# Closing groups of rows inside a symmetric attention layer instead of after it

## The chip, the cores and the metric

The kernel runs on one core of one Trainium2 chip. The metric is the device time of one execution in microseconds (us), taken as the median of several runs. TensorE is called PE, VectorE DVE, ScalarE ACT, GpSimd POOL and SyncE SP, as the profile does. Matmuls are in fp32, and each shows as two records (two passes); a transpose through PE is one pass.

## The reference

Four images of 64 x 64 pixels and 64 channels go through four layers:

```python
x = _L0_conv_ref(x, ...)   # attention over 4096 pixels, q = xWq, k = xWk, v = xWv
x = _L1_conv_ref(x, ...)   # norm, pointwise, depthwise 3x3, gates, residuals
x = _L2_conv_ref(x)        # attention without weights, see below
x = _L3_conv_ref(x, ...)   # non-local block: theta, phi, g of 32 channels, batch norm, residual
```

Layer 2 reads its input as `B, C, H, W = x.shape`, so what it takes for channels is the image's first spatial axis and its tokens are the 64 x 64 pairs of the last two axes:

```python
xf = x.reshape(B, C, N)
scores = jnp.einsum('bci,bcj->bij', xf, xf)
attn = jax.nn.softmax(scores, axis=-1)
out = jnp.einsum('bcj,bij->bci', xf, attn).reshape(B, C, H, W)
return out + x
```

Its score matrix is symmetric: query and key are the same vectors. Layer 3 is

```python
f = jax.nn.softmax(jnp.einsum('bnd,bmd->bnm', theta_x, phi_x), axis=-1)
y = jnp.einsum('bnm,bmd->bnd', f, g_x).reshape(B, H, W, INNER)
w_y = jnp.einsum('bhwd,dc->bhwc', y, w_W) + w_b
return x + w_y_normalised_over_batch_and_pixels
```

so the normalisation needs all four images, and the finish comes after the last of them.

## The kernel before

One list of items is built for the whole program, and a driver emits item after item. Each item writes its instructions into the engines' queues, so the order in the list is the order on every engine; engines wait for each other by semaphores. Beside the items there are three ways to insert work: `at(i, fn)` emits a function after item i; generators under `conv` and `misc` emit one step whenever the items' declared times (`conv.tick`, `misc.tick`) have added up to what the step asks by its `yield`; and `small` emits a function within an item of layer 3.

The order of the stages is: layer 0 of four images, with layer 1 spread between; layer 2 of image 0 in its full form; then in turn the symmetric layer 2 of an image (72 items) and layer 3 of the image before it (64 items); last, layer 3 of images 2 and 3 back to back, and the finish. All intermediate results stay on the chip.

**Symmetric layer 2** (`layer2s`). The 4096 tokens form eight groups of 512. A block is the scores of one group against another. Since the matrix is symmetric, a block between two different groups is computed once and used twice. `SIDES` says which group h does the blocks with which other groups, two at a time (a pair, four items). An item is one 128 x 1024 half of such a block: `score` (PE, L1432, into a two-bank slot of PSUM), the exponentials with row sums (ACT, L1437), and for a block off the diagonal a 32 x 32 block transpose (DVE, `turned`, L1449) and column sums (POOL, L1460). `products` (PE, L1484) come two items later; after a pair, `turned_products` (PE, 128 records, L1500) use the transposed half with weights loaded by 16 SP DMAs per group (`weights`, L1415), and DVE adds the result into the accumulator `A` (`add_to`, L1474). Scores rotate over three slots of two banks each; two more banks hold the products. `spread_sums` (DVE, L1468, L1469) turns POOL's column sums.

When all 72 items are done, an image is closed: `close2s` sums the row sums and column sums of all groups (four matmuls L1550, DVE L1552 to L1556), transposes `A` through PE (four times eight transposes, L1561) and adds the scaled result to `X` on DVE (L1562, L1568). Its five steps are inserted at items 8, 12, 22, 32 and 42 of the next image's symmetric layer; for image 3, as a generator in layer 3 of image 2. Image 0 is closed by `close2`, from item 2 of image 1's symmetric layer on, DVE only (L1372 to L1379).

**Layer 3.** `open3` makes theta (L1588), phi (L1599) and g (L1607), each into a slot of two banks, and `keys3` spreads phi by 16 SP DMAs (L1622). An item of `layer3` is 16 score records (L1643) into four banks of seven that rotate, exponentials on ACT (L1654), and products two items later (L1700) into the eighth bank. Denominators are summed on DVE (L1691) or, for eight items in each half of 32, by POOL's accumulating DMAs (L1671, L1673). After each half come `totals` (L1712, L1736) and a reciprocal (L1728 to L1730), and then `close` with the projection (L1750), ACT (L1763) and statistics (L1765). `features2` (L1300, L1303) transposes the next image's `X` for its layer 2, in two parts of eight transposes, each in two banks.

Of the kernel before, what the change touches and what calls it, by code (L numbers as in the profile page):

```python
# [691 lines left out]
def fast_path(ctx: ExitStack, tc: tile.TileContext, a: dict, out: bass.AP, bad):  # L692
# [42 lines left out]

    def take_slots(*slots):
        turn_of["slots"], turn_of["ps"], turn_of["banks"] = list(slots), 0, 0
# [144 lines left out]
    sel4 = const.tile([128, 32], F32, name="sel4")  # L882
    pwb = const.tile([128, 2, 2], F32, name="pwb")
# [22 lines left out]
    def setup():  # L906
# [33 lines left out]
        for i in range(4):  # L940
# [5 lines left out]
            yield 4.0  # L946
        nc.vector.tensor_add(sel4, ident[:, 0:32], ident[:, 32:64])
# [345 lines left out]
    def features2(b):  # L1293
# [3 lines left out]
        for g in range(2):  # L1297
            ps = new_ps()
            for i in range(8):
                nc.tensor.transpose(ps[:, bass.ts(i, 128)], x[:, bass.ts(8 * g + i, 128)], ident)  # L1300
            for e, copy in enumerate((nc.vector.tensor_copy, nc.scalar.copy)):
                own, other = slice(64 * e, 64 * e + 64), slice(64 - 64 * e, 128 - 64 * e)
                copy(kv[own, bass.ts(g, 8), e, :], ps[own, :].rearrange("p (a n) -> p a n", n=128))  # L1303
                nc.sync.dma_start(out=kv[other, bass.ts(g, 8), e, :], in_=kv[own, bass.ts(g, 8), e, :])
            yield 7.0

    def layer2(b):
# [7 lines left out]
        def scores(n):  # L1315
# [3 lines left out]
            for jb in range(4 * (n % 8), 4 * (n % 8) + 4):  # L1319
# [13 lines left out]
                conv.tick(2.3)  # L1333
# [51 lines left out]
    SIDES = [[(7, (h + 1) % 7), ((h + 2) % 7, (h + 3) % 7)] for h in range(7)] + [[]]  # L1385

    def layer2s(b, when_free):
# [7 lines left out]
        for h in (7, 0, 1, 2, 3, 4, 5, 6):  # L1395
# [3 lines left out]
                for pi, pair in enumerate(SIDES[h]) for gi, g in enumerate(sorted(pair)) for u in range(2)  # L1399
            ]  # L1400
            steps += other + own if h == 6 else own + other
        st = {"e": {}, "T": {}, "esum": {}}

        def slot(g, t):
            k = used[g, t] = used.get((g, t), -1) + 1
            c = 16 * g + 4 * t if g < 7 else 112 + 8 * t
            return m.zs[:, c + k : c + k + 1]
# [34 lines left out]
        def turned(n):  # L1442
# [3 lines left out]
            if ti == 0 and pi not in st["T"]:  # L1446
                st["T"][pi] = new_big("turned")
            T = st["T"][pi].rearrange("p (e s j) -> p s e j", e=16, s=8)
# [4 lines left out]
        def column_sums(n):  # L1453
# [7 lines left out]
            if (pi, ti) == (1, 3):  # L1461
# [30 lines left out]
        def turned_products(h, pi):  # L1492
            T, slots = st["T"][pi], [new_ps(), new_ps()]
# [11 lines left out]
            for i in range(2):  # L1505
                for gi, g in enumerate(sorted(SIDES[h][pi])):
# [11 lines left out]
        def item(n):  # L1518
            h = steps[n][0]
            if n >= 4 and steps[n - 4][0] == h and (n == 4 or steps[n - 5][0] != h):  # L1520
                weights(h)
# [11 lines left out]
            if n - 2 in last_of:  # L1533
                turned_products(*last_of[n - 2])
                if last_of[n - 2] == (6, 0):
                    when_free()
            if n - 5 in last_of and last_of[n - 5][1] == 1:
                spread_sums(last_of[n - 5][0])

# [5 lines left out]
    def close2s(b):  # L1545
# [509 lines left out]
```

## Time and profile before

| | us |
|---|---|
| median of 3 runs (2470.71 to 2475.36) | 2475.31 |
| the profiled execution | 2475.64 |
| its span | 2473.9 |
| PE busy in the span | 2431.5 (98%) |
| ACT busy | 1642.7 (66%) |
| DVE busy | 1428.7 (58%) |
| POOL busy | 506.8 (20%) |

Stages, in us from the span's start: layers 0 and 1 to about 1016; layer 2 of image 0 to 1271; symmetric layer 2 of image 1 from 1274 to 1474, layer 3 of image 0 to 1611, symmetric layer 2 of image 2 to 1808, layer 3 of image 1 to 1946, symmetric layer 2 of image 3 to 2143, layer 3 of image 2 to 2300, layer 3 of image 3 to about 2443, and the finish.

How to read it: shares are of the whole span, and a stage can have another bound than the sum. "Idle before" names what ended an engine's idleness. A group's mean is of one instruction; matmuls run beside each other on parts of the array, so the distance from one start to the next is a better price than the length. The granted clock is the TensorE clock that the throttle let through, 1.00 being full speed; over the whole span it was 0.996.

### The profile page before, as it was taken

The page shows a single profiled execution, that of the slowest core. Times are in us where ns is not written, and L with a number is a line of the kernel's source. Part 1 is how long each engine was busy: PE and PEld are TensorE (multiplying, and loading weights), DVE is VectorE, ACT ScalarE, POOL GpSimd, SP SyncE. Part 2 cuts the span into 40 slices and gives each one's busy share as a digit, 9 for nine tenths or more (in the row PEclk, how much of TensorE's full clock was granted, in tenths as well). Part 3 has the DMA queues.
Part 4 walks back from the last instruction along what each step waited for, and adds up shares of the span by engine and source line. Part 5 has one row for each costly group of instructions (what it writes and reads, how often), then busy time and mean ns, then how long its engine had stood idle before and what let it go on. Part 6 is the DMA issues. An engine that isn't in the chain of part 4 may idle for free.

```text
span 2473.9 us, 62215 instructions
## 1 busy us (share of the span) xinstructions
PE 2431.5 (98%) x27037; PEld 925.5 (37%) x27037; DVE 1428.7 (58%) x1701; ACT 1642.7 (66%) x2979; POOL 506.8 (20%) x345
## 2 busy tenths in 40 slices
PE   9999999999999999999989999999999999999998
PEld 3343453336433643344324442134431244421123
DVE  2010277228822782267335558877668876687886
ACT  4666766667666766666645459954479744569996
POOL 2000000000000000000007661256631366512110
PEclk9999999999999999999999999999999999999999
DMA  3000000010000000000000027610075400376554
GB/s 79 1 18 1 18 1 18 18 19 1 18 18 18 1 18 18 18 2 18 18 18 19 19 48 151 138 27 21 18 148 116 81 21 22 73 139 127 118 118 119
DMA packets 59151, 115.33 MB, mean 47 GB/s; under 512 B 11149, under 2 KB 30326, under 8 KB 58870
## 3 DMA queue, kind: packets, MB, share of 16 engines
q0 software_dynamic: 19136, 67.68, 13.7%
q1 hardware_dynamic: 38981, 41.75, 7.5%
q8 instruction: 214, 3.51, 0.6%
q10 hardware_dynamic: 752, 1.85, 0.2%
q14 instruction: 68, 0.55, 0.1%
HBM read 4.80 MB, written 4.19 MB: 4 GB/s over the span
## 4 chain that ended last, share of the span: by engine, by line
PE 88%; DVE 5%; ACT 4%; DMA 1%; issue 1%; SPq 0%; POOL 0%; DVEq 0%; ACTq 0%; POOLq 0%
PE PS L1116 18%; PE PS L1090 17%; PE PS L1643 8%; PE PS L1700 8%; PE PS L1432 7%; PE PS L1484 7%; PE PS L1500 6%; PE PS L1323 4%; PE PS L1343 4%; PE PS L1200 2%; DVE tg L1691 2%; ACT e L1654 2%; DMA xn<-e 1%; ACT e L1095 1%; PE PS L1165 1%
## 5 line engine op out<-in xcount | busy, mean ns | idle before, releaser
L1095 ACT ACTIVATE e<-PS 128x1024 f32<-128x1024 f32 x512 | 523.7, 1023 | 331.3 <-PE PS L1090 299.2
L1116 PE MATMUL PS<-e,vq 64*64 64x512 f32 x4096 | 573.8, 591 | 0.0
L1090 PE MATMUL PS<-X,q 64*64 64x512 f32 x4096 | 571.6, 591 | 1.8 <-DVE X L974 1.7
L1654 ACT ACTIVATE e<-PS 128x512 f32<-128x512 f32 (+2 forms) x593 | 500.4, 915 | 66.9 <-PE PS L1643 42.8
L1437 ACT ACTIVATE e<-PS 128x512 f32<-128x512 f32 x432 | 253.5, 594 | 289.6 <-PE PS L1432 270.9
L1691 DVE TENSOR_TENSOR tg<-tg,e 128x2048 f32<-128x2048 f32 x174 | 398.6, 2291 | 49.4 <-ACT e L1654 37.0
L1233 DVE SCALAR_TENSOR_TENSOR y<-pad,vec,y 128x1024 f32<-128x1024 f32 x240 | 308.1, 1284 | 7.5
L1460 POOL TENSOR_TENSOR esum<-esum,e 128x1024 f32<-128x1024 f32 x126 | 298.9, 2372 | 58.6 <-ACT e L1437 51.5
L1643 PE MATMUL PS<-tg,ph 32*64 32x512 f32 x4096 | 300.3, 615 | 6.5 <-DVE A L1474 3.3
L1090 PEld LDWEIGHTS PS<-X,q 64*64 64x64 f32 x4096 | 184.4, 133 | 257.3 <-issue 178.8
L1116 PEld LDWEIGHTS PS<-e,vq 64*64 64x64 f32 x4096 | 184.6, 133 | 251.3 <-issue 152.9
L1700 PE MATMUL PS<-e,tg 128*32 128x512 f32 x2048 | 273.5, 606 | 0.0
L1449 DVE STREAM_TRANSPOSE turned<-e 128x1024 f32<-128x1024 f32 x168 | 206.7, 1239 | 79.8 <-ACT e L1437 79.7
L1484 PE MATMUL PS<-e,X 64*64 64x512 f32 x1728 | 232.7, 594 | 6.2 <-DVE A L1474 6.1
L1432 PE MATMUL PS<-ko 64*64 64x512 f32 x1728 | 235.4, 598 | 0.0
L1528 POOL MEMSET A<- 128x4096 f32 x3 | 11.2, 3736 | 1012.5 <-PE PS L1116 1012.5
L1103 DVE TENSOR_REDUCE sums<-zs 128x1 f32<-128x4 f32 x128 | 19.6, 153 | 301.3 <-ACT e L1095 300.9
L1331 ACT ACTIVATE e<-PS 128x1024 f32<-128x1024 f32 x128 | 129.6, 1023 | 83.7 <-PE PS L1323 80.4
L1500 PE MATMUL PS<-turned,xn 32*64 32x256 f32 x5376 | 157.2, 377 | 2.5 <-DVE sums L1554 1.6
L1673 POOL DMA_DIRECT2D xn<-e x112 | 97.6, 906 | 294.4 <-ACT e L1654 201.1
L1474 DVE TENSOR_TENSOR A<-PS,A 128x256 f32<-128x256 f32 (+1 forms) x216 | 92.5, 477 | 105.2 <-PE PS L1500 80.7
L1643 PEld LDWEIGHTS PS<-tg,ph 32*64 32x64 f32 x4096 | 65.4, 130 | 227.7 <-ACT e L1654 175.8
(224 smaller groups left out, 1927.4 us busy)
## 6 DMA issues: line engine op xcount, KB each, us to landing
xn<-e POOLq DMA_DIRECT2D x128, 512.0 KB, 5.3
xn<-X SPq DMA_DIRECT2D x336, 32.0 KB
xn<-t SPq DMA_DIRECT2D x64, 128.0 KB
ph<-tg SPq DMA_DIRECT2D x64, 128.0 KB
ko<-ko SPq DMA_DIRECT2D x16, 256.0 KB
xr<-in_x_dram SPq DMA_DIRECT2D x13, 256.0 KB
q<-q SPq DMA_DIRECT2D x12, 256.0 KB
out_dram<-o SPq DMA_DIRECT2D x7, 256.0 KB
```

What stands on the lines that cost most here:

```text
L1090: mm(ps[64 * c : 64 * c + 64, bass.ts(r, 512)], m.q[rows_, 128 * t + 64 * c : 128 * t + 64 * c + 64], x[rows_, bass.ts(g, 512)], start=Tru ...
L1095: act(es[g // 2][:, bass.ts(g % 2, 1024)], ps, AF.Exp, bias=SHIFT0, accum_out=zs[:, g : g + 1],)
L1116: ins = mm(PS[64 * s : 64 * s + 64, 2048 + 512 * j : 2560 + 512 * j], vq[rows_, :], es[j // 2][rows_, k : k + 512], start=t == 0 and i < 2 ...
L1233: stt(y1, win, wt, y1, ALU.mult, ALU.add)
L1432: mm(ps[64 * c : 64 * c + 64, bass.ts(r, 512)], m.ko[rows_, k : k + 64], m.ko[rows_, bass.ts(h, 512)], start=True, stop=True,)
L1460: nc.gpsimd.tensor_add(esum, st["e"][n - 1] if (pi, ti) == (0, 1) else esum, st["e"][n])
L1484: mm(st["acc"][r][64 * c : 64 * c + 64, :], xw[rows_, jb, :], st["e"][n][rows_, bass.ts(c, 512)], start=n == mine[0], stop=n == mine[-1],)
L1500: mm(slots[q // 2][64 * c : 64 * c + 64, o : o + 256], st["xr"][rows_, w : w + 64], T[rows_, bass.ts(e, 256)], start=e < 2, stop=e >= 14,)
L1643: mm(PS[64 * c : 64 * c + 64, bass.ts(banks[k], 512)], m.ph[32 * k : 32 * k + 32, 128 * mc + 64 * c : 128 * mc + 64 * c + 64], m.th[32 * k ...
L1654: act(e[:, 512 * lo : 512 * k], PS[:, 512 * banks[lo] : 512 * banks[lo] + 512 * (k - lo)], AF.Exp,)
L1691: nc.vector.tensor_add(esum, esum, e)
L1700: mm(st["y"][32 * k : 32 * k + 32, :], m.gx[:, i % 32, :], es[i][:, bass.ts(k, 512)], start=mc == 0, stop=i % 32 == 31,)
```

## The change

**Pairs.** `SIDES` is another table: groups 0 to 3 each do blocks with groups 4 to 7 and so finish earlier; there are still 28 blocks off the diagonal in 14 pairs. `COUNT` and `FIRST` lay out the row sums by group.

**Closing by groups.** `close2s` is replaced by `close_group(b, g)`, eight calls per image. Its first step sums the group's row sums on DVE and, for seven of the eight groups, column sums by four small matmuls into columns 256 to 260 of one PSUM piece, which DVE adds. Then four matmuls of `A` with `fold2` go into columns 0 to 256 of the same piece: `fold2` is two stacked 64 x 64 identities, so that a transpose and the sum of the two halves are one matmul. DVE scales and adds into `X`, four times 64 columns. Groups 1, 0, 2, 3 and 5 are closed within the image's own symmetric layer (items 38, 50, 53, 61 and 71), groups 4, 6 and 7 at items 6, 9 and 12 of the next image's, or, for image 3, in layer 3 of image 2.

**Insertions in one bank.** `piece()` gives one bank in layer 3 (and half a slot elsewhere). `open3`, `close`, `features2` and `totals` take pieces: theta in two, phi in two, g in two, close in two halves, features in four. In layer 3 they are emitted right after an item's exponentials, cut 1024 + 1024 there, not 512 + 1536 (`between3`, `cut`).

**Smaller moves.** `weights` is issued in the item before a group begins; `close2(0)` moves from item 2 to items 16, 17, 30 and 31 of image 1's symmetric layer; `conv.tick` in layer 2 is 2.5 instead of 2.3.

The core of the diff:

```diff
...
+    def piece():
+        if turn_of["banks"]:
+            return PS[:, bass.ts(new_bank(), 512)]
+        return new_ps()[:, 0:512]
+
     def take_slots(*slots):
...
     sel4 = const.tile([128, 32], F32, name="sel4")
+    fold2 = const.tile([128, 64], F32, name="fold2")
     pwb = const.tile([128, 2, 2], F32, name="pwb")
...
             yield 4.0
+        nc.vector.tensor_add(fold2, ident[:, 0:64], ident[:, 64:128])
         nc.vector.tensor_add(sel4, ident[:, 0:32], ident[:, 32:64])
...
         kv = ko[:, 0:N].rearrange("p (a e n) -> p a e n", e=2, n=128)
-        for g in range(2):
-            ps = new_ps()
-            for i in range(8):
-                nc.tensor.transpose(ps[:, bass.ts(i, 128)], x[:, bass.ts(8 * g + i, 128)], ident)
+        for g in range(4):
+            ps = piece()
+            for i in range(4):
+                nc.tensor.transpose(ps[:, bass.ts(i, 128)], x[:, bass.ts(4 * g + i, 128)], ident)
             for e, copy in enumerate((nc.vector.tensor_copy, nc.scalar.copy)):
                 own, other = slice(64 * e, 64 * e + 64), slice(64 - 64 * e, 128 - 64 * e)
-                copy(kv[own, bass.ts(g, 8), e, :], ps[own, :].rearrange("p (a n) -> p a n", n=128))
-                nc.sync.dma_start(out=kv[other, bass.ts(g, 8), e, :], in_=kv[own, bass.ts(g, 8), e, :])
-            yield 7.0
+                copy(kv[own, bass.ts(g, 4), e, :], ps[own, :].rearrange("p (a n) -> p a n", n=128))
+                nc.sync.dma_start(out=kv[other, bass.ts(g, 4), e, :], in_=kv[own, bass.ts(g, 4), e, :])
+            yield 3.5
...
                 follow(0)
-                conv.tick(2.3)
+                conv.tick(2.5)
                 misc.tick(1.8)
...
-    SIDES = [[(7, (h + 1) % 7), ((h + 2) % 7, (h + 3) % 7)] for h in range(7)] + [[]]
+    SIDES = [
+        [(1, 3), (4, 5), (6, 7)], [(2, 3), (4, 5), (6, 7)], [(0, 3), (4, 5), (6, 7)], [(4, 5), (6, 7)],
+        [(5, 7)], [(6, 7)], [(4, 7)], [],
+    ]
+    COUNT = [1 + sum(g in pair for sides in SIDES for pair in sides) for g in range(8)]
+    FIRST = [4 * sum(COUNT[:g]) for g in range(8)]
...
                 (h, g, u, pi, 2 * gi + u)
-                for pi, pair in enumerate(SIDES[h]) for gi, g in enumerate(sorted(pair)) for u in range(2)
+                for pi, pair in enumerate(SIDES[h]) for gi, g in enumerate(pair) for u in range(2)
             ]
...
         st = {"e": {}, "T": {}, "esum": {}}
+        begin = [next(n for n in range(72) if steps[n][0] == h) for h in range(7)]
+        begin[0] = 2
+        run_of = {k: i for i, k in enumerate((h, pi) for h in range(8) for pi in range(len(SIDES[h])))}
+        closed = {
+            begin[2] + 8: 1, begin[3] + 6: 0, begin[3] + 9: 2, begin[5] + 1: 3, begin[6] + 5: 5,
+        }
...
             h = steps[n][0]
-            if n >= 4 and steps[n - 4][0] == h and (n == 4 or steps[n - 5][0] != h):
-                weights(h)
+            if n == 6:
+                weights(0)
+            if n + 1 in begin[2:] or n == 8:
+                weights(1 if n == 8 else begin.index(n + 1))
             score(n)
...
                 turned_products(*last_of[n - 2])
-                if last_of[n - 2] == (6, 0):
+                if run_of[last_of[n - 2]] == 12:
                     when_free()
-            if n - 5 in last_of and last_of[n - 5][1] == 1:
+            if n - 5 in last_of and last_of[n - 5][1] == len(SIDES[last_of[n - 5][0]]) - 1:
                 spread_sums(last_of[n - 5][0])
+            if n in closed:
+                close_group(b, closed[n])
...
-    def close2s(b):
+    def close_group(b, g):
         x, m = X[:, b], im[b]
-        ps = new_ps()
-        cs = m.cs.rearrange("p (j k) -> p j k", k=4)
-        for k in range(4):
-            mm(ps[32 * k : 32 * k + 32, 0:28], sel4, cs[:, 0:28, k], start=True, stop=True)
-        tot = sums2[:, b, :]
-        nc.vector.tensor_reduce(tot[:, 0:28], m.zs[:, 0:112].rearrange("p (j k) -> p j k", k=4), AX.X, ALU.add)
-        nc.vector.tensor_reduce(tot[:, 28:32], m.zs[:, 112:144].rearrange("p (j k) -> p j k", k=8), AX.X, ALU.add)
-        nc.vector.tensor_add(tot[:, 0:28], ps[:, 0:28], tot[:, 0:28])
-        rz = sm.tile([128, 32], F32, tag="rz2", name="rz2")
+        ps, tot = piece(), sums2[:, b, 4 * g : 4 * g + 4]
+        nc.vector.tensor_reduce(
+            tot, m.zs[:, FIRST[g] : FIRST[g] + 4 * COUNT[g]].rearrange("p (t k) -> p t k", t=4), AX.X, ALU.add
+        )
+        if SIDES[g]:
+            cs = m.cs.rearrange("p (j k) -> p j k", k=4)
+            for k in range(4):
+                mm(
+                    ps[32 * k : 32 * k + 32, 256:260], sel4, cs[:, 4 * g : 4 * g + 4, k],
+                    start=True, stop=True,
+                )
+            nc.vector.tensor_add(tot, ps[:, 256:260], tot)
+        rz = sm.tile([128, 4], F32, tag="rz4", name="rz4")
         nc.vector.reciprocal(rz, tot)
-        yield 2.0
-        for i in range(4):
-            ps, t = new_ps(), new_t()
-            for j in range(8):
-                nc.tensor.transpose(ps[:, bass.ts(j, 128)], m.A[:, 1024 * i + 128 * j : 1024 * i + 128 * j + 128], ident)
-            nc.vector.tensor_mul(
-                t.rearrange("p (j n) -> p j n", n=128), ps.rearrange("p (j n) -> p j n", n=128),
-                rz[:, bass.ts(i, 8)].unsqueeze(2).to_broadcast([128, 8, 128]),
-            )
-            xs = x[:, bass.ts(i, 512)].rearrange("p (j h) -> p j h", h=H)
-            for o in range(2):
-                nc.vector.tensor_add(xs, xs, t.rearrange("p (j o h) -> p j o h", j=8, o=2)[:, :, o, :])
-            yield 3.0
+        for t in range(4):
+            c = 512 * g + 128 * t
+            mm(ps[:, bass.ts(t, 64)], m.A[:, c : c + 128], fold2, start=True, stop=True)
+        for t in range(4):
+            xs = x[:, bass.ts(4 * g + t, 64)]
+            stt(xs, ps[:, bass.ts(t, 64)], rz[:, t : t + 1], xs, ALU.mult, ALU.add)
...
     BY_DMA = (2, 5, 8, 11, 14, 17, 20, 23)
-    small = {}
+    small, between3 = {}, {}
     held = []
...
         m.gx = m.tg[:, 1024:2048].rearrange("p (t d) -> p t d", d=32)
-        ps = new_ps()
         for nb in range(2):
+            ps = piece()
             for jj in range(2):
...
                     mm(
-                        ps[32 * k : 32 * k + 32, bass.ts(nb, 512)], thw[64 * s : 64 * s + 64, :],
+                        ps[32 * k : 32 * k + 32, :], thw[64 * s : 64 * s + 64, :],
                         tok(x, s, 2 * nb + jj), start=True, stop=True,
                     )
-        nc.vector.tensor_scalar_add(m.th, ps, V("L3_conv_theta_b"))
-        yield 3.5
-
-        ps, own = new_ps(), m.tg[:, 2048:3072].rearrange("p (s n) -> p s n", s=2)
-        m.own = own
-        for j in range(4):
+            nc.vector.tensor_scalar_add(m.th[:, bass.ts(nb, 512)], ps, V("L3_conv_theta_b"))
+            yield 3.0
+
+        m.own = own = m.tg[:, 2048:3072].rearrange("p (s n) -> p s n", s=2)
+        for s in range(2):
+            ps = piece()
+            for j in range(4):
+                mm(
+                    ps[32 * j : 32 * j + 32, :], phw[64 * s : 64 * s + 64, :],
+                    tok(x, s, j), start=True, stop=True,
+                )
+            nc.vector.tensor_scalar_add(own[:, s, :], ps, V("L3_conv_phi_b"))
+            yield 3.0
+        for i in range(2):
+            ps = piece()
+            for t in range(8):
+                mm(ps[:, bass.ts(t, 64)], x[:, bass.ts(8 * i + t, 128)], gw, start=True, stop=True)
             for s in range(2):
-                mm(
-                    ps[32 * j : 32 * j + 32, bass.ts(s, 512)], phw[64 * s : 64 * s + 64, :],
-                    tok(x, s, j), start=True, stop=True,
-                )
-        nc.vector.tensor_scalar_add(own, ps.rearrange("p (s n) -> p s n", s=2), V("L3_conv_phi_b"))
-        yield 3.5
-        ps = new_ps()
-        for t in range(16):
-            mm(ps[:, bass.ts(t, 64)], x[:, bass.ts(t, 128)], gw, start=True, stop=True)
-        for s in range(2):
-            nc.vector.tensor_add(
-                m.gx[:, bass.ts(s, 16), :],
-                ps.rearrange("p (t s d) -> p t s d", s=2, d=32)[:, :, s, :],
-                gb.unsqueeze(1).to_broadcast([128, 16, 32]),
-            )
-        yield 3.5
+                nc.vector.tensor_add(
+                    m.gx[:, 16 * s + 8 * i : 16 * s + 8 * i + 8, :],
+                    ps.rearrange("p (t s d) -> p t s d", s=2, d=32)[:, :, s, :],
+                    gb.unsqueeze(1).to_broadcast([128, 8, 32]),
+                )
+            yield 3.0
...
-            exp(0, 1)
+            cut = 2 if first + n in between3 else 1
+            exp(0, cut)
             if mc == 1 and (nb or last):
...
             else:
-                exp(1, 4)
+                exp(cut, 4)
+            for fn in between3.get(first + n, []):
+                fn()
             if mc in BY_DMA:
...
         def totals(n):
-            k = new_bank()
-            z = PS[:, bass.ts(k, 512)]
+            z = piece()
             sums(z, True)
...
-        def project(yz, ps, c0, cols):
+        def project(yz, ps, c0, cols, halves=(0, 1)):
             for k in range(4):
-                s, jj = k // 2, k % 2
-                mm(
-                    ps[64 * s : 64 * s + 64, 512 * jj : 512 * jj + c0], wo[32 * k : 32 * k + 32, :],
-                    yz[32 * k : 32 * k + 32, cols], start=True, stop=True,
-                )
-
-        def close(nb):
-            if b % 2 == 0 and nb == 0:
+                if k % 2 in halves:
+                    o = 512 * halves.index(k % 2)
+                    mm(
+                        ps[64 * (k // 2) : 64 * (k // 2) + 64, o : o + c0], wo[32 * k : 32 * k + 32, :],
+                        yz[32 * k : 32 * k + 32, cols], start=True, stop=True,
+                    )
+
+        def close(nb, i):
+            if b % 2 == 0 and nb == 0 and i == 0:
                 wys["pair"] = new_big("wy") if b else new_pad("wy")
-            if nb == 0:
+            if nb == 0 and i == 0:
                 wys[b] = wys["pair"][:, bass.ts(b % 2, 2048)]
-            ps = new_ps()
-            project(st["yz"], ps, 512, slice(0, 512))
-            wy = wys[b][:, bass.ts(nb, 1024)]
+            ps = piece()
+            project(st["yz"], ps, 512, slice(0, 512), (i,))
+            wy = wys[b][:, 1024 * nb + 512 * i : 1024 * nb + 512 * i + 512]
             act(wy, ps, AF.Identity, bias=V("L3_conv_w_b"))
-            for i in range(2):
-                nc.vector.bn_stats(bst[:, b, nb, i, :], wy[:, bass.ts(i, 512)])
+            nc.vector.bn_stats(bst[:, b, nb, i, :], wy)
...
             elif n % 32 == 31:
-                at(first + n + (5 if n == 63 and b < 2 else 4), lambda n=n: totals(n))
-                at(first + n + 11, lambda n=n: close(n // 32))
+                ends = [(5 if n == 63 and b < 2 else 4, lambda n=n: totals(n))]
+                ends += [(11 + 2 * i, lambda n=n, i=i: close(n // 32, i)) for i in range(2)]
+                for i, fn in ends:
+                    if n == 63 and b < 2:
+                        at(first + n + i, fn)
+                    else:
+                        between3[first + n + i] = [fn]
...
             if b == 1:
-                misc_from[f + 2] = [close2(0)]
+                turns = close2(0)
+                for i in (16, 17, 30, 31):
+                    at(f + i, lambda turns=turns: next(turns))
             else:
-                turns = close2s(b - 1)
-                for i in (8, 12, 22, 32, 42):
-                    at(f + i, lambda turns=turns: next(turns))
+                for i, g in ((6, 4), (9, 6), (12, 7)):
+                    at(f + i, lambda b=b, g=g: close_group(b - 1, g))
             misc_from[f + 46] = [open3(b - 1)]
...
             if b + 1 < B:
-                misc_from[f + 3] = [features2(b + 1)]
+                turns = features2(b + 1)
+                for i in (4, 7, 10, 13):
+                    between3[f + i] = [lambda turns=turns: next(turns)]
     f = len(items)
-
-    def keys_of_last():
-        keys3(B - 1)
-        yield 3.5
-
-    misc_from[f - 56] = [close2s(B - 1), open3(B - 1), keys_of_last()]
+    for i, g in ((-58, 4), (-56, 6), (-54, 7)):
+        between3[f + i] = [lambda g=g: close_group(B - 1, g)]
+    turns = open3(B - 1)
+    for i in range(6):
+        between3[f - 52 + 2 * i] = [lambda turns=turns: next(turns)]
+    at(f - 44, lambda: keys3(B - 1))
     misc_to[f] = True
...
```

## The prediction

> **What bounds the kernel now.** I read the page's shares first, then the chain of work that ended last, then the waits of TensorE (PE), and only then single stages in the timeline.
>
> ```profile
> PE 2431.5 (98%) x27037; PEld 925.5 (37%) x27037; DVE 1428.7 (58%) x1701; ACT 1642.7 (66%) x2979; POOL 506.8 (20%) x345
> PE 88%; DVE 5%; ACT 4%; DMA 1%; issue 1%; SPq 0%; POOL 0%; DVEq 0%; ACTq 0%; POOLq 0%
> ```
>
> PE is the bound nearly everywhere: what is added to PE is paid in full, and so is every stop of PE. The profiled execution took 2475.64 us, its span 2473.9 plus 1.7 around it; the median of the runs is 2475.31, so the sum is made on 2475.6. What PE waits for today is little:
>
> ```profile
> PE PS L1484 <- DVE A L1474: 6.1, 1, 6.1
> PE PS L1643 <- DVE A L1474: 3.3, 3, 1.5
> PE PS L1643 <- ACT e L1654: 2.9, 2, 2.5
> PE PS L1500 <- DVE sums L1554: 1.6, 2, 0.8
> ```
>
> Columns: total us, times, longest. The first lies at the start of symmetric layer 2 of image 1, the 2.5 in layer 3 of image 2. Now an ordinary item of symmetric layer 2 (timeline; start, length):
>
> ```profile
> 1693.59 1.04 PE L1432 MATMUL PS<-ko 64*64 64x512 f32 x8
> 1694.45 1.04 PE L1484 MATMUL PS<-e,X 64*64 64x512 f32 x8
> 1695.26 0.59 ACT L1437 ACTIVATE e<-PS 128x512 f32<-128x512 f32 x1
> 1695.31 1.04 PE L1432 MATMUL PS<-ko 64*64 64x512 f32 x8
> 1695.97 1.25 DVE L1449 STREAM_TRANSPOSE turned<-e 128x1024 f32<-128x1024 f32 x1 [0.41 <-ACT e L1437]
> ...
> 1697.13 1.09 PE L1561 MATMUL PS<-ident,A 128*128 128x128 f32 x8
> 1698.16 1.09 PE L1432 MATMUL PS<-ko 64*64 64x512 f32 x8
> ```
>
> The reader is to see two things. PE's item lasts 1.72 (score 0.86, products 0.86). VectorE (DVE) ends the transpose of the score begun at 1693.59 only at 1697.22, 3.63 later: DVE runs about two items behind PE, which costs nothing as long as PE needs nothing fresh from it. And one old insertion (eight transposes) makes its item 1.13 longer.
>
> **The change part by part.** *The waiting fold, the main term.* In the changed kernel as built, each close of a group with column sums issues on PE four sum matmuls, then four fold matmuls into the same bank. The first fold waits for DVE's add of the column sums, because add and fold touch one bank. DVE is in order, and in front of that add stands the transpose of the very item whose score PE has just issued. Prices: sum matmuls 0.32 (0.22 from start to the next score at L1550, and 0.10 for switching); the fold's eight passes (fp32, two each) by L1607 below, 32 passes in 3.71 us, so 0.93, and 0.2 for switching, together 1.14. The ends are 0.93 and 1.2.
>
> ```profile
> 1741.56 3.79 PE L1607 MATMUL PS<-gw,X 128*128 128x64 f32 x32
> 1745.27 0.21 PEld L1432 LDWEIGHTS PS<-ko 64*64 64x64 f32 x8
> ```
>
> Closes after an item with a transpose (groups 1, 0, 2; items 38, 50, 53): PE is ready for the fold 0.86+0.86+0.32 = 2.04 after its score; the add ends at 3.63 + 0.14 (reduce) + 0.19 (add) + 0.05 = 4.02. PE stands 2.0, then folds, and the next score starts at 5.16 instead of 1.72: +3.45. Queued behind the waiting fold is all of PE, the next score first, and so ACT's exponentials and DVE's next transpose.
>
> Closes right after turned products (groups 3, 5; items 61, 71; group 6 in the next stage): DVE first does the four additions into A.
>
> ```profile
> 1691.97 1.42 DVE L1474 TENSOR_TENSOR A<-PS,A 128x256 f32<-128x256 f32 x4 [1.98 <-PE PS L1500]
> ```
>
> The fold starts about 1.9 after the turned products instead of 0.32: a stop of 1.6, and +3.05 with the work. Per image 3 x 3.45 + 2 x 3.05 = 16.45; three images: **+49.4**.
>
> *Closes at the start of the next symmetric stage* (items 6, 9, 12 there, two stages). Group 4 at item 6 meets a DVE that is far behind with layer 3's totals:
>
> ```profile
> 1610.12 9.48 DVE L1691 TENSOR_TENSOR tg<-tg,e 128x2048 f32<-128x2048 f32 x4
> 1627.36 2.73 DVE L1730 SCALAR_TENSOR_TENSOR yz<-inv,yz 128x512 f32<-128x512 f32 x1
> 1630.01 4.61 DVE L1449 STREAM_TRANSPOSE turned<-e 128x1024 f32<-128x1024 f32 x4
> ```
>
> Item 6's transpose is the second of the four and ends near 1632.4; PE would be ready about 1627.2: a stop of 5.5, +7.0. Group 6 +3.05; group 7 has no column sums and no wait, +1.2. Removed: four insertions of eight transposes at 1.13, the old sum matmuls 0.32, and PE's two waits behind them, which cost that item 2.1. Net 11.25 - 6.95 = 4.3 each, **+8.7**.
>
> *Split insertions.* A piece still takes two passes of its matmuls, though fewer tiles share a pass. Phi's 16 records take 1.02 from start to next score (L1599, 1738.66 to 1739.68); split, twice that, and 0.3 more for gw: +1.5 for three images, **+4.5**. Close in halves, seven times 1.0 to 1.2 less what L3(2) takes in below: **+6.5**. Four pieces of features for two: **+1.9**. Lower end for all three: zero, if half the tiles take half the time.
>
> *What gets better.* Image 1's symmetric layer begins with DVE in close2(0) and the first T late; the scores of items 4 and 7 are 15.6 apart, where 3 scores and 5 products make 6.9. The change puts close2(0) at items 16 to 31: I leave 1.5 of the 8.8: **-7.3**. Cover of the layer-3 start waits (1.5, 0.9): **-1.6**. Layer 3 of image 2 carries 25.8 us above 64 items of 2.04; about 15 is inserted PE work, 10.6 is waiting and slow clock. Closes there are early and keys' DMAs (16 on SP, sharing the engines with POOL's accumulations) come sooner; folds wait 0.5 where DVE is idle. Between -2 and -10: **-6**. Sharing the pairs anew leaves 28 blocks, 56 transposes, 56 POOL additions: zero, hidden or not. The four DVE updates of X per close replace 13 us of DVE work per image and follow the fold: zero, as nothing waits for them before three items later; if that cover fails, 0.2 each.
>
> *Moved DMAs and ticks.* The 16 SP loads of a group's turned weights move from its fifth item to the item before its first, ahead of nothing else on SP in that stage but close by close; they land in the DMA engines' idle time (share 0.12 to 0.13 in these stages) and are needed some eight items later: zero, and if late, as long as the load, at most 11 us per stage by SP's row of 18 issues at 1285.74. DVE's update of X must wait until these loads have read X; they are then long done. Features for two issue eight half-size DMAs on SP instead of four: zero, hidden by layer 3. The conv tick of 2.5 instead of 2.3 spends layer 1's DVE work a little sooner within layer 2, where DVE is busy 121 of 255 us: zero. Exponentials of 1024+1024 for 512+1536 columns at a close in layer 3: ACT is busy 128 of 137 us there, one more start-up of some 0.2, hidden by the inserted PE work.
>
> Sum: 49.4 + 8.7 + 4.5 + 6.5 + 1.9 - 7.3 - 1.6 - 6 = **+56**.
>
> *The clock.* PE's two long waits are followed by half speed (columns: us, busy of PE, PEld, DVE, ACT, POOL, granted clock, DMA, GB/s):
>
> ```profile
> 2220.66:2224.07 3.41, 1.55 (x18) 0.21 (x10) 0.39 (x2) 0.03 (x1) 0.00 (x0) 1.00 0.14 32
> 2224.07:2227.48 3.41, 2.79 (x14) 0.49 (x14) 3.31 (x2) 3.41 (x5) 0.00 (x0) 0.50 0.00 0
> 2227.48:2230.90 3.42, 3.42 (x28) 0.53 (x24) 3.32 (x2) 0.80 (x2) 0.00 (x0) 0.50 0.00 0
> 1471.00:1478.00 7.00, 5.45 (x96) 2.09 (x88) 2.18 (x6) 1.94 (x2) 0.00 (x0) 1.00 0.40 90
> ```
>
> A stretch of 3.41 us with PE busy for 1.55 was followed by 6.83 us at 0.50, worth at most 3.4 us, about 3.2. The wait of 1.55 us within 1471 to 1478 was not. So between 1.55 and 1.9 us of idleness within one such stretch lies the switch. New stops: two of 5.5 (surely), nine of 2.0 (a half: a stretch must hold nearly all of it), eight of 1.6 (a quarter): 2 + 4.5 + 2 = 8.5 times 3.2: **+27**; ends 6 and 60.
>
> The Trainium skill, page "TensorE: Matmul & The Clock Gate", Part 1, speaks of a return to the slow state after at least one idle window of about 3.4 us. By that only the two long stops would switch, +6.4, and the sum would be 2538; the row above, where 1.86 us of idleness was enough, speaks for more.
>
> 2475.6 + 56 + 27 = **2558**.
>
> **Rivals.** (a) *The stops come, the clock holds* for all but the long ones: 2475.6 + 56 + 6 = 2538; for it, the 1.5 us wait left the clock alone; against it, the row above. (b) *Nearly all stops switch the clock*: 19 x 3.2 = 61, 2592. (c) *Stops half as long*, because DVE gains on PE after every stop and insertion: -21 and few switches, 2515 or so. Against: transposes are released by ACT, not by DVE's queue. (d) *No stop at all, and not slower.* Place: the 19 waiting folds; if the add ran ahead of the transpose, 9 x 2.0 + 8 x 1.6 + 2 x 5.5 = 42 and all the clock go: 2490. This decides the sign only once the PE work left, +14, falls under 5, which the lower ends (pieces at half the time: -11) would do: 2479, and with layer 3 of image 2 at -10, 2475. Against: the order on DVE is fixed as built.
>
> **How the numbers follow.** Forecast (6 to 14 switches, 2548 to 2578) 0.48; (a) 0.22; (b) 0.09; (c) 0.13; (d) 0.08, of which faster 0.03, within 0.2% (5 us, about what a measurement of this kernel can tell from no change) 0.02, the rest slower. Range: leaving out the outer half of (b) and (d) with a little of (c), 2505 to 2592; the forecast's own range is 2540 to 2580. Faster 0.03, same 0.02, slower 0.95.
>
> **What would show it.** PE's list of waits should be headed by the fold (L1586) on DVE's sums (L1581), 19 to 21 times, some 42 us in all, longest near 5.5. Granted clock of 0.5 in about eight further spots behind these, and a mean clock near 0.99. Symmetric stages about 220 to 230 us instead of 196, the first of them some 210; layer 3 of image 2 about 150 instead of 156. The prediction is wrong if the fold's wait is short (then look at whether the transposes end sooner after the score than 3.6), if half-clock spots are absent, or if layer 3 of image 2 or the start of image 1's layer moves by more than ten.

## The result and the profile after

The changed kernel takes 2552.36 us (median of 4 runs, 2550.04 to 2554.5) against 2473.31 before: ratio 1.032, 95% interval 1.0302 to 1.0338. The profiled execution has a span of 2551.9 us. The page's shares, then the chain that ended last:

```profile
PE 2478.0 (97%) x27277; PEld 942.5 (37%) x27277; DVE 1426.3 (56%) x1843; ACT 1646.0 (65%) x2984; POOL 507.4 (20%) x345
...
PE 90%; DVE 4%; ACT 4%; issue 1%; DMA 0%; DVEq 0%; SPq 0%; ACTq 0%
```

PE still carries the chain. It has 46.5 us more of busy time and 31.5 us more of idleness than before (73.9 against 42.4). The waits of PE in the changed kernel (total us, times, longest; four lines of the list):

```profile
PE PS L1586 <- DVE sums L1581: 42.6, 21, 4.9
...
PE PS L1363 <- ACT ko L1310: 1.7, 1, 1.7
...
PE PS L1503 <- DVE A L1493: 1.3, 1, 1.3
PE PS L1664 <- DVE X L1589: 1.0, 1, 1.0
```

The first line is the fold (L1586) behind DVE's add of the column sums (L1581), the wait that the prediction put in its place: 19 times 1.7 to 4.9 us, and twice 0.3 in layer 3 of image 2. The old waits of 6.1 (products on A), 3.3 and 2.9 us are gone or down to 1.3 and 1.0. One close in the timeline (item 38 of image 1; start, length):

```profile
1377.38 1.09 PE L1450 MATMUL PS<-ko 64*64 64x512 f32 x8
...
1379.26 0.24 PE L1577 MATMUL PS<-cs,sel 128*32 128x4 f32 x8
...
1379.88 1.25 DVE L1468 STREAM_TRANSPOSE turned<-e 128x1024 f32<-128x1024 f32 x1 [0.94 <-ACT e L1455]
...
1381.05 0.12 DVE L1571 TENSOR_REDUCE sums<-zs 128x4 f32<-128x8 f32 x1
1381.27 0.16 DVE L1581 TENSOR_TENSOR sums<-PS,sums 128x4 f32<-128x4 f32 x1
...
1381.58 1.08 PE L1586 MATMUL PS<-fold,A 128*128 128x64 f32 x8 [2.08 <-DVE sums L1581]
...
1382.59 1.09 PE L1450 MATMUL PS<-ko 64*64 64x512 f32 x8
```

PE has its column sums done at about 1379.5. DVE first does the item's transpose, then reduces and adds, and the fold starts at 1381.58, 4.20 after the score. The next score comes 5.21 after this one instead of 1.72.

Stage by stage, in us between the first scores of the stages:

| stage | before | after | difference |
|---|---|---|---|
| to layer 2 of image 0 | 1016.5 | 1017.3 | +0.8 |
| layer 2 of image 0 | 257.8 | 262.6 | +4.8 |
| symmetric layer 2, image 1 | 199.5 | 213.1 | +13.6 |
| layer 3, image 0 | 137.6 | 140.0 | +2.4 |
| symmetric layer 2, image 2 | 197.1 | 227.9 | +30.8 |
| layer 3, image 1 | 138.0 | 138.3 | +0.3 |
| symmetric layer 2, image 3 | 197.1 | 227.4 | +30.3 |
| layer 3, image 2 | 156.3 | 149.0 | -7.3 |
| layer 3, image 3, and the finish | 174.0 | 176.3 | +2.3 |

The clock behind the waits, in the windows view (us, busy of PE, of PE's weight loads, of DVE, ACT and POOL, granted clock, DMA share, GB/s):

```profile
1377.69:1381.10 3.41, 1.82 (x24) 0.46 (x16) 2.48 (x6) 1.27 (x4) 3.05 (x2) 1.00 0.00 0
1381.10:1384.52 3.42, 2.94 (x28) 1.79 (x32) 1.27 (x8) 0.79 (x3) 1.24 (x1) 1.00 0.00 0
1432.31:1435.72 3.41, 1.49 (x24) 0.59 (x15) 2.60 (x5) 1.27 (x4) 3.33 (x2) 1.00 0.00 0
1435.72:1439.13 3.41, 3.41 (x19) 1.82 (x21) 0.86 (x4) 0.17 (x1) 2.49 (x2) 0.50 0.00 0
```

The wait of 2.08 us at item 38 falls over two stretches of 3.41 us, and the clock stays. The wait of 1.92 us at item 53 falls into one, PE is busy for 1.49 us of it, and the next stretch is at half speed. In every kernel here the tail, the last 5.6 to 8.8 us of the span, is at half speed too. Outside it there are twelve such spots, eight of 3.41 us and four of 6.83, 54.6 us in all, against two and 13.7 us before. At half speed 54.6 us hold at most 27.3 us of lost time.

### The profile page after: what moved, and what is told of

Its sections match the earlier page's. It is cut to its first block, busy times and chain, and to the rows that moved or that the text cites. A ratio compares the mean times of both kernels' runs of the same rounds, so it can differ in the third digit from the quotient of the medians.

```text
span 2551.9 us, 62945 instructions
## 1 busy us (share of the span) xinstructions
PE 2478.0 (97%) x27277; PEld 942.5 (37%) x27277; DVE 1426.3 (56%) x1843; ACT 1646.0 (65%) x2984; POOL 507.4 (20%) x345
## 4 chain that ended last, share of the span: by engine, by line
PE 90%; DVE 4%; ACT 4%; issue 1%; DMA 0%; DVEq 0%; SPq 0%; ACTq 0%
PE PS L1123 17%; PE PS L1097 17%; PE PS L1664 9%; PE PS L1724 8%; PE PS L1450 8%; PE PS L1503 7%; PE PS L1519 6%; PE PS L1350 4%; PE PS L1330 4%; PE PS L1207 2%; DVE tg L1715 2%; ACT e L1675 1%; PE PS L1586 1%; ACT e L1455 1%; ACT e L1102 1%
## 5 line engine op out<-in xcount | busy, mean ns | idle before, releaser
L1102 ACT ACTIVATE e<-PS 128x1024 f32<-128x1024 f32 x512 | 524.2, 1024 | 331.3 <-PE PS L1097 299.9
L1664 PE MATMUL PS<-tg,ph 32*64 32x512 f32 x4096 | 294.3, 613 | 1.1 <-DVE X L1589 1.0
L1450 PE MATMUL PS<-ko 64*64 64x512 f32 x1728 | 244.2, 624 | 0.0
L1503 PE MATMUL PS<-e,X 64*64 64x512 f32 x1728 | 239.2, 613 | 1.6 <-DVE A L1493 1.3
L1664 PEld LDWEIGHTS PS<-tg,ph 32*64 32x64 f32 x4096 | 63.5, 129 | 219.3 <-ACT e L1675 179.6
```

The lines of the kernel that those rows point to most:

```text
L1102: act(es[g // 2][:, bass.ts(g % 2, 1024)], ps, AF.Exp, bias=SHIFT0, accum_out=zs[:, g : g + 1],)
L1450: mm(ps[64 * c : 64 * c + 64, bass.ts(r, 512)], m.ko[rows_, k : k + 64], m.ko[rows_, bass.ts(h, 512)], start=True, stop=True,)
L1503: mm(st["acc"][r][64 * c : 64 * c + 64, :], xw[rows_, jb, :], st["e"][n][rows_, bass.ts(c, 512)], start=n == mine[0], stop=n == mine[-1],)
L1664: mm(PS[64 * c : 64 * c + 64, bass.ts(banks[k], 512)], m.ph[32 * k : 32 * k + 32, 128 * mc + 64 * c : 128 * mc + 64 * c + 64], m.th[32 * k ...
```

## The experiments

The theory: the fold's wait, with the half clock that follows it, makes most of the loss; the rest is added PE work. The rivals: the wait has another cause; the clock has little part in it; DVE's lateness comes back elsewhere.

**The fold ahead of the column sums.** Same work, same bank:

```diff
+        for t in range(4):
+            c = 512 * g + 128 * t
+            mm(ps[:, bass.ts(t, 64)], m.A[:, c : c + 128], fold2, start=True, stop=True)
         if SIDES[g]:
             cs = m.cs.rearrange("p (j k) -> p j k", k=4)
...
-        for t in range(4):
-            c = 512 * g + 128 * t
-            mm(ps[:, bass.ts(t, 64)], m.A[:, c : c + 128], fold2, start=True, stop=True)
```

> The changed kernel, but a close issues its four fold matmuls ahead of the four column-sum matmuls. Same work, same bank; the fold no longer stands behind DVE's add. Theory (the wait of the fold on the add, and the half clock that follows these waits, make most of the loss): PE's wait of L1586's matmuls on DVE falls from 42.6 us in 21 waits to under 5, the spots of half clock outside the tail fall from 12 to at most 2, and the time falls by 42 for the waits and about 20 for the clock, to 2490 (2483 to 2498). Rival 1 (the clock has little to do with these waits): the waits go, the spots stay, 2510. Rival 2 (DVE's lateness comes back elsewhere, as a wait of scores for a PSUM slot that the fold's result still holds): new waits of scores on DVE's L1589 of 20 us or more, 2520 or above.

Measured 2491.4 us, ratio to before 1.0076 (1.0059 to 1.0093). The same item in its timeline:

```profile
1377.14 1.09 PE L1450 MATMUL PS<-ko 64*64 64x512 f32 x8
...
1379.02 1.11 PE L1576 MATMUL PS<-fold,A 128*128 128x64 f32 x8
...
1379.63 1.25 DVE L1468 STREAM_TRANSPOSE turned<-e 128x1024 f32<-128x1024 f32 x1 [0.94 <-ACT e L1455]
...
1380.05 0.24 PE L1580 MATMUL PS<-cs,sel 128*32 128x4 f32 x8
...
1380.22 1.09 PE L1450 MATMUL PS<-ko 64*64 64x512 f32 x8
```

The fold now starts while DVE has not begun the transpose, and the item takes 3.08 us. In this kernel's list of waits of PE the fold does not appear; the entries on DVE's update of X (L1589) are

```profile
PE PS L1450 <- DVE X L1589: 2.9, 2, 1.4
...
PE PS L1664 <- DVE X L1589: 2.0, 1, 2.0
```

so rival 2 has 4.9 us of such waits, 1.0 of them old, not 20. One half-clock spot of 3.41 us is left outside the tail: rival 1 falls too. The gain of 61 us is 42.6 of waits, less 3.9 that came back, and (54.6 - 3.4) / 2 = 25.6 of clock, together 64; the spans differ by 63.5.

**The close ahead of the item's transpose.** At items 38, 50 and 53 only:

```diff
...
             score(n)
+            if n in closed and n not in last_items:
+                close_group(b, closed[n])
             turned(n)
...
-            if n in closed:
+            if n in closed and n in last_items:
                 close_group(b, closed[n])
```

> The changed kernel, but at items 38, 50 and 53 the close is issued right after the item's score, ahead of the item's own DVE transpose. Bank and wait stay as they are. Theory (the add stands in DVE's queue behind that transpose): the nine waits of 1.9 to 2.1 us at these items fall to about 1.1 at item 53, 0.8 at item 38 and 0.4 at item 50, together from 18 to 7; the other twelve waits stay; with four to six fewer spots of half clock 2530 (2522 to 2540). Rival (the wait is the round trip of sums, add and semaphore, whatever stands in front): waits of 2.0 as before, 2552.

Measured 2534.07, ratio to before 1.0249 (1.0232 to 1.0266). The waits are 31.3 us in 21 instead of 42.6, and at item 38:

```profile
1378.14 1.42 DVE L1493 TENSOR_TENSOR A<-PS,A 128x256 f32<-128x256 f32 x4 [1.98 <-PE PS L1519]
...
1379.72 0.16 DVE L1584 TENSOR_TENSOR sums<-PS,sums 128x4 f32<-128x4 f32 x1
...
1380.03 1.08 PE L1589 MATMUL PS<-fold,A 128*128 128x64 f32 x8 [0.78 <-DVE sums L1584]
```

The wait is 0.78 where it was 2.08, and what is left is behind the additions into A. At items 50 and 53 it is 0.3 and 1.1, close to what was expected. With bank and semaphore unchanged, it is what stands in front of the add in DVE's queue that makes the wait.

**Group 4 later.**

```diff
-                for i, g in ((6, 4), (9, 6), (12, 7)):
+                for i, g in ((9, 6), (12, 7), (20, 4)):
```

> The changed kernel with the closing of group 4 moved from item 6 to item 20 of the next symmetric layer (two places). Theory (its wait of 4.9 us is DVE's backlog of layer 3's totals): at item 20 it waits 2.0 like the other closes behind a transpose, the two long half-clock spots of 6.8 us at these places go or become short, and the old wait at item 9 (1.2) may come back: 2552 - 2 x 1.7 - 2 to 6 = 2544 (2540 to 2550). Rival (group 4 waits for something of its own): 4.9 again, 2552.

Measured 2553.42 against the changed kernel's 2552.36: the expected gain did not come. At item 6 of the changed kernel DVE comes to the add only behind the end of layer 3's totals and the transposes that had queued up (timeline, DVE):

```profile
1648.89 2.71 DVE L1754 SCALAR_TENSOR_TENSOR yz<-inv,yz 128x512 f32<-128x512 f32 x1
1651.52 2.36 DVE L1468 STREAM_TRANSPOSE turned<-e 128x1024 f32<-128x1024 f32 x2
...
1654.04 0.16 DVE L1581 TENSOR_TENSOR sums<-PS,sums 128x4 f32<-128x4 f32 x1
```

With the close moved, the wait of 4.9 us did go from item 6, so group 4 waits for nothing of its own, but at item 20 it is 3.3. DVE there:

```profile
1693.60 1.25 DVE L1468 STREAM_TRANSPOSE turned<-e 128x1024 f32<-128x1024 f32 x1 [0.52 <-ACT e L1455]
1694.76 0.67 DVE L1487 STREAM_TRANSPOSE esum<-esum 128x512 f32<-128x512 f32 x1
1695.54 0.69 DVE L1488 TENSOR_REDUCE cs<-esum 128x16 f32<-128x512 f32 x1
1696.14 0.17 DVE L1571 TENSOR_REDUCE sums<-zs 128x4 f32<-128x24 f32 x1
```

The expectation forgot that item 20 also spreads POOL's column sums: two more instructions, 1.4 us, in front of the add. The turned products' old wait came back (1.6 in two), and the half clock outside the tail was 58.0 us instead of 54.6, at other items. 3.3 us less waiting, 1.6 back, 1.7 of clock: nothing.

**The split insertions alone, on the kernel before** (features in four pieces, theta, phi and g in two, the projection in halves; for example):

```diff
-        ps, own = new_ps(), m.tg[:, 2048:3072].rearrange("p (s n) -> p s n", s=2)
...
+        for s in range(2):
+            ps = piece()
+            for j in range(4):
+                mm(
+                    ps[32 * j : 32 * j + 32, :], phw[64 * s : 64 * s + 64, :],
```

> The kernel before with only the split insertions (features in four, theta, phi and g in two, the projection in two halves), at the old places. Theory (a piece with half of the tiles takes as long as the whole did): four splits of phi and g at 1.5, one theta in layer 3 at 1.0, seven projections at 1.0 to 1.2, features 1.9 to 4: 2475 + 17 = 2490 (2484 to 2496). Rival (half of the tiles take half of the time): 2475 to 2479.

Measured 2485.0, ratio 1.005 (1.0033 to 1.0067): 12.7 us. Phi in the changed kernel (timeline, PE) shows why:

```profile
1407.81 1.06 PE L1619 MATMUL PS<-X,phw 64*32 64x512 f32 x8
1408.80 1.09 PE L1450 MATMUL PS<-ko 64*64 64x512 f32 x8
...
1410.68 1.06 PE L1619 MATMUL PS<-X,phw 64*32 64x512 f32 x8
1411.67 0.66 PE L1450 MATMUL PS<-ko 64*64 64x512 f32 x4
```

Each half of 8 records takes 0.99 us, as the whole of 16 did (1.02). One wait is new: the transposes in layer 2 behind ACT's copy of a features piece, 2.2 us here and 1.7 in the changed kernel.

**Fold first, with whole insertions** (the first experiment's kernel, its insertions made whole again at the places of their first pieces), for example:

```diff
-                ends += [(11 + 2 * i, lambda n=n, i=i: close(n // 32, i)) for i in range(2)]
+                ends += [(11, lambda n=n: close(n // 32))]
...
-                for i in (4, 7, 10, 13):
+                for i in (4, 10):
...
-    for i in range(6):
-        between3[f - 52 + 2 * i] = [lambda turns=turns: next(turns)]
+    for i in range(3):
+        between3[f - 52 + 4 * i] = [lambda turns=turns: next(turns)]
```

> The changed kernel with the fold ahead of the column sums and with whole insertions (features in two, theta, phi, g and the projection as one piece each, in the places of their first pieces). Theory (what is left of the loss with the fold ahead is the split, about 13, and the fold's own PE work): 2491 - 13 = 2478 (2475 to 2482). Rival (whole insertions of two banks hold up the exponentials of layer 3, which is what the pieces avoid): 2486 or above.

Measured 2483.68, ratio 1.0048 (1.0031 to 1.0065): 7.7 less than with pieces, between theory and rival. A new half-clock spot of 6.83 us, worth up to 3.4, came with it at the start of layer 3 of image 1; without it some 2480. So pieces cost. What is left over the kernel before is 10.0 us (2473.69 in the same measurement). The fold's own PE work has a large part in it: the symmetric layers of images 2 and 3 have no half clock in either kernel and take 200.7 us each here against 197.1 before, 3.6 more for the eight closes in place of the old insertions. The prediction's prices for such a layer, without the stops, come to 4.5.

**Image 0's closing moved.** Two parts of the change, on the kernel before:

```diff
-                conv.tick(2.3)
+                conv.tick(2.5)
...
-                misc_from[f + 2] = [close2(0)]
+                turns = close2(0)
+                for i in (16, 17, 30, 31):
+                    at(f + i, lambda turns=turns: next(turns))
```

> The kernel before with only the closing of image 0 moved to items 16, 17, 30 and 31 of image 1's symmetric layer, and the conv tick of 2.5 in layer 2. Theory (the wait of 6.1 us of L1484 on DVE and the half clock after it come from DVE being late with that close): the wait falls to about 1.3, the half clock at that place goes, 2468 (2465 to 2471). Rival (layer 1's work moves into layer 2 and costs there what it gains here): no change, 2474.

Measured 2476.68, ratio 1.0019 (1.001 to 1.0029): the theory's 6 us did not come. The same with the old tick:

> The kernel before with image 0's closing at items 16, 17, 30 and 31 as in the change, but with the conv tick of before (2.3). It tells which of the two moves of the change gave the gain back. If the tick did: layer 2 of image 0 stays at 257.8 us as before (261.4 with the tick of 2.5), 2469 to 2472. If the places did: two waits of turned products on DVE's transposes, 5.6 us together, stay, and with them a spot of half clock; both can hold, then about 2470. Rival (the tick is harmless): layer 2 at 261 as with it, 2476.

Measured 2475.51, ratio 1.0009 (0.9999 to 1.0018). Its waits of PE:

```profile
PE PS L1500 <- DVE turned L1449: 5.6, 2, 3.2
...
PE PS L1484 <- DVE A L1474: 1.2, 1, 1.2
```

The old wait fell from 6.1 to 1.2, and 5.6 us came back as turned products waiting for transposes behind two steps of the closing in a row. So the places did it. The tick moved about 3.6 us of layer 1's work: layer 2 takes 261.4 with it and 257.8 without, the symmetric layer 197.9 and 201.4. At other places, each step right after turned products:

```diff
-                misc_from[f + 2] = [close2(0)]
+                turns = close2(0)
+                for i in (9, 13, 19, 23):
+                    at(f + i, lambda turns=turns: next(turns))
```

> The kernel before with only the closing of image 0 moved, here to items 9, 13, 19 and 23 of image 1's symmetric layer, each right after turned products, and with the conv tick of before (2.3). Theory (what the run with items 16, 17, 30 and 31 lost was its place, two steps in a row ahead of transposes that turned products wait for, and layer 1's work moved by the tick): PE's wait of 6.1 us falls to about 1.3, no half clock, no new waits on transposes, that symmetric layer 199.5 to 192.5 us, total 2466 (2463 to 2469). Rival (DVE in that stretch has too much to do wherever the steps stand): the wait comes back as waits of turned products on DVE, 2471 to 2473.

Measured 2467.02, ratio 0.9973 (0.9964 to 0.9983). The symmetric layer takes 194.5 us instead of 199.5, 2 more than expected, since 1.7 us of waits on transposes remain.

**Layer 3 of image 2 rearranged, on the kernel before.**

```diff
-    misc_from[f - 56] = [close2s(B - 1), open3(B - 1), keys_of_last()]
+    turns = close2s(B - 1)
+    for i in range(5):
+        at(f - 58 + 2 * i, lambda turns=turns: next(turns))
+    turns3 = open3(B - 1)
+    for i in range(3):
+        at(f - 48 + 2 * i, lambda turns=turns3: next(turns))
+    at(f - 43, lambda: keys3(B - 1))
```

> The kernel before with only layer 3 of image 2 rearranged: the five steps of image 3's closing at items 6 to 14, theta, phi and g at items 16, 18 and 20, keys' DMAs at item 21, all whole as before. Theory of the prediction (keys' 16 DMAs come late and share the DMA engines with POOL's accumulations, so that PE waits 2.5 us for an exponential and goes to half clock): that layer 3 takes 148 to 150 us instead of 156, no half clock there, 2467 (2465 to 2470). Rival (the 2.5 us wait was a chance of the one profiled execution, since two kernels with other changes show 152 there): no gain beyond 1, 2472.

Measured 2469.55, ratio 0.9987 (0.9977 to 0.9997); the stage takes 150.4 us instead of 156.3. Both sides had a part: the kernel with the closing of image 0 at items 9 to 23 has this stage unchanged, has the 2.5 us wait again and takes 152.8, because the clock held (windows view):

```profile
2214.55:2217.97 3.42, 2.23 (x26) 0.37 (x18) 1.06 (x1) 0.20 (x1) 0.00 (x0) 1.00 0.29 65
2217.97:2221.38 3.41, 2.05 (x22) 0.41 (x22) 2.58 (x2) 2.70 (x4) 0.00 (x0) 1.00 0.00 1
2221.38:2224.79 3.41, 3.41 (x48) 0.73 (x48) 3.31 (x2) 3.31 (x5) 0.00 (x0) 1.00 0.03 5
```

Here the wait lies over two stretches, in the profiled execution of before it lay in one. Nor is the wait itself there every time: with this stage as before, it is 2.5 us in three profiled executions (the kernel before, and the closing of image 0 at items 9 to 23 and, with the old tick, at 16 to 31), but at most 0.9 in the run with the tick of 2.5, where the stage takes 152.2. That keys' DMAs make the wait, by sharing the DMA engines with POOL's accumulations, was not tested by itself: this run moved the closing, theta, phi and g as well.

**Both moves together:** the last two diffs in one kernel.

> The two moves of the runs before this one together, on the kernel before. Theory: their gains add up, 2472 - 7 - 5 = 2460 (2457 to 2465). Rival (both gains were chance or are given back): 2470 or above.

Measured 2465.02, ratio 0.9964 (0.9952 to 0.9977): the fastest of all, by 8.7 us against the kernel before. No half clock is left outside the tail. The gains do not add up fully (6.7 and 4.1).

## Why the prediction was right

The prediction said 2558 us and slower; measured were 2552.36, or +79.1 between the medians against a sum of +83 on the profiled execution. The mechanism is the one that it named; that the clock's part came out so close is luck. Its steps:

- *The waiting fold.* Predicted 42 us of waits in 19 places, 2.0 behind a transpose, 1.6 after turned products, 5.5 for group 4. Measured 42.6 in 21, with 2.08, 1.97 and 1.92 behind a transpose, 1.72 to 1.82 after turned products, 4.93 and 4.94 for group 4. The extra item time at item 38 is 3.49 against 3.45. The first two experiments show the cause; rival (d), all waits gone, had 2490, and the fold issued first gives 2491.4.
- *The clock.* Predicted 8.5 spots at 3.2 us, 27 us. Measured 12 spots, eight of them only 3.41 us long, at most 27.3 us. The sum was right by two errors: more waits switched the clock (both of group 4, all six at items 50 and 53, both at item 9, one of three each at items 61 and 71, none at 38), and most cost less, as PE came back after one stretch.
- *Group 4 at item 6.* The cause named, DVE's backlog of layer 3's totals, is right; the wait was 0.6 shorter.
- *Split insertions.* Predicted 4.5 + 6.5 + 1.9 = 12.9; alone, on the kernel before, they cost 12.7. Not foreseen was the 1.7 to 2.2 us wait behind ACT's copy in layer 2.
- *Image 0's closing.* Predicted -7.3 as a gain of the move itself. The wait did fall to 1.3 in the changed kernel. But on the old pair order the same places give back 5.6 us as another wait, and the changed kernel has no such wait, so the gain hangs on the rest of the change, most likely on the new pairs, where the turned products fall at other items; that was not tested. With the fold first and whole insertions that layer takes 198.1 us instead of 199.5, though it holds five closes of some 1.4 us that it did not hold before; less the tick's 3.6 the move is worth some 5 us there, an estimate. The step named what the wait was, and did not ask what would be late next.
- *The conv tick.* Priced at zero. It shifts 3.6 us from the first symmetric stage to layer 2, most of layer 2's 4.8, and the two runs that differ in it alone are 1.2 us apart, within their intervals.
- *Layer 3 of image 2.* Predicted -6, measured -7.3. About 3.5 of it is the half clock that the profiled execution of before had (156.3 against 152.8 with the same wait and no half clock); the sum was made on that execution, and so took in a gain which not every execution offers.
- *Start of layer 3.* Predicted -1.6; the 3.3 us of waits became 1.0.
- *Exponentials of 1024 + 1024 columns.* The extra start-up of 0.2 does not arise: 512 + 1536 are two instructions as well.

The rule behind the count, a switch between 1.55 and 1.9 us of idleness in a stretch, was read from a row that does not carry it. The 1.55 us within 1471 to 1478 lie across two stretches of the grid that the half-clock spots keep to, and neither stretch holds all of it (the kernel before):

```profile
1469.72:1473.14 3.42, 2.55 (x96) 1.87 (x80) 0.80 (x3) 0.00 (x0) 0.58 (x1) 1.00 0.91 201
1473.14:1476.55 3.41, 2.73 (x32) 1.02 (x32) 0.62 (x2) 1.60 (x2) 0.00 (x0) 1.00 0.25 56
```

The last section has what the runs show instead.

Of the rivals, (a) is refuted by the twelve spots, (b) by the seven waits that kept the clock, (c) by waits of full length, (d) as built by the 42.6 us of waits; with the fold first its price is met.

## What to carry to other kernels

When an engine that bounds the kernel is made to wait for a small fresh result of another engine, price the wait by what stands in front of that result in the other engine's queue, not by the result's own 0.2 us. Here the fold writes other columns than the add reads, and yet waited for it: in this kernel two results in one PSUM bank were ordered as if they were one. Issue first what needs no answer, and the wait is gone at no cost in work. Whether sums in a bank of their own would do the same was not tried. Before a move is credited with the stop it removes, look at what the moved work will stand in front of at its new place.

## What the runs showed of the hardware

All half-clock spots within one execution begin on one grid of 3.413 us, and outside the tail last one or two steps of it. So a wait of 2.5 us switched the clock in one kernel and not in another, by where it lay on the grid. How busy PE is in a stretch goes far to tell what follows. Of the stretches at full clock between the first score of layer 2 and the last of layer 3, in all twelve profiles, take those without any matmul on the whole 128 x 128 array. With PE busy for 1.55 us or less every one was followed by half speed, with 1.60 or more none, but for one of 2.02 in the run with the close ahead of the transpose.

The Trainium skill's page "TensorE: Matmul & The Clock Gate", Part 1, has the grid and its length, and these runs agree; it puts the fall to the slow state after at least one idle window, and here a window with PE busy for nearly half of it was enough, so the measurement decides.

Stretches that do hold matmuls on the whole array do not fit busy time (changed kernel, windows view):

```profile
1418.65:1422.07 3.42, 2.50 (x22) 2.50 (x23) 1.80 (x8) 0.00 (x0) 1.78 (x1) 1.00 0.00 0
1422.07:1425.48 3.41, 3.41 (x20) 1.26 (x19) 0.76 (x2) 0.79 (x3) 0.00 (x0) 0.50 0.02 5
1787.29:1790.70 3.41, 2.14 (x19) 2.14 (x20) 2.15 (x8) 0.00 (x0) 2.12 (x1) 1.00 0.01 2
1790.70:1794.11 3.41, 3.41 (x19) 1.92 (x22) 0.76 (x2) 0.14 (x1) 0.00 (x0) 0.50 0.02 5
```

Here PE counts 2.50 and 2.14 us as busy and the clock still fell. These stretches hold the fold and part of g and nothing else, matmuls of only 64 columns whose weight loads keep PE's load side busy for just as long. The kept traces have five such stretches, with PE busy for 1.65 to 2.50 us, and all five were followed by half speed; two others that were full of such matmuls (3.41 us) were not. So it looks as if such matmuls count for the clock, but for less than their busy time says. No run varied this alone, and it stays a guess.
